# Finer interleaving slices for attention and the expert mixtures in a one-core hybrid scan kernel

## The chip, the cores and the metric

The kernel runs on one core of one Trainium2 chip. The metric is the device time of one execution in microseconds, the median of several runs. The engines are called PE (TensorE), ACT (ScalarE), DVE (VectorE), POOL (GpSimd) and SP (SyncE, which here only issues DMAs).

## The reference, cut to what matters

Four images of 32 x 32 tokens with 256 channels go through four layers. Each token row is called t, L is 1024 tokens per image.

```python
x = L0(x)                    # norm, 256->512, depthwise 3x3, gelu, scan with 64 states, norm, 512->256
x = L1(x)                    # 1x1, grouped 3x3, 1x1, residual
t = t + L2_attn(_ln_t(t))    # 8 heads of 32, masked softmax over scores, values, projection, norm
t = t + L2_ffn(_ln_t(t))     # mixture: 8 experts, hidden 256, top 2
t = t + L3_attn(_ln_t(t))    # projections, scan with 16 states, gate, projection
t = t + L3_ffn(_ln_t(t))     # mixture: 8 experts, hidden 512, top 2
# both scans:     h = exp(dt * A) * h + (dt * x) * B ;  y = sum over states of h * C
# both mixtures:  h = gelu(x @ w1[e] + b1[e]) ;  out += combine[:, e] * (h @ w2[e] + b2[e])
```

All experts are computed for all tokens; the weights of the experts that a token did not choose are zero.

## The kernel before, in words

**Two programs woven into one.** The scans are the backbone. `scans` walks through 1280 units of 128 rows (channel and state) by 1024 steps, in the order of the list `SCANS`: the 64-state scan of an image has 256 units, the 16-state scan has 64. Everything else (fronts, back ends, convolutions, attention, mixtures) is "side work": generators that yield after each small piece, called a tick. `STAGES` lists the side stages and the scan that each must wait for. The mixture of layer 2 and the attention lie in `middle`, the mixture of layer 3 in `last`.

**What one unit does.** All scan instructions are recorded through a helper and carry line 120 in the profile. For unit k: a DMA broadcasts the rows of dt into a tile `dA` (issued four units ahead), ACT turns it into a decay by `Exp` (two units ahead), PE spreads the input over the states into PSUM `ps_rep` (two matmuls, one unit ahead, two buffers of two banks each), DVE multiplies `ps_rep` by B in place, DVE runs the scan into `h`, and POOL multiplies `h` by C. Every second unit, PE sums the states of two units into `ps_y` (four matmuls in four column groups).

**Who decides the order.** The program is written with a manual schedule: each engine executes its instructions in the order in which the Python code records them. `scans` yields twice per unit: after the multiplication by B and after the scan. I call the time between two yields a half-unit slot; there are 2568 of them. In each slot `run` advances the side work by at most `TICKS = 2` ticks, and stops earlier when the planner's own clock of any engine is ahead of its clock of DVE. The planner keeps that clock with a table of costs (`Metered.COST`), which each recorded instruction adds to; an engine that is behind DVE by more than `LAG = 4` us is lifted. The costs that generators yield are not used: `advance` only asks whether a tick was made. If a scan needs a stage that is not finished, `need` runs side work at once, without scan units in between, until it is.

**The pipeline helper.** `pipe(items, *steps)` runs each item through its steps with an offset of one tick per step, the later step first: with two steps, a tick records step two of the item before and then step one of the item at hand, and then yields once.

**Attention.** `heads` (called once per half of the queries and pair of heads, eight times per image) pipes eight key blocks through `scores` and `values`. `scores` records six matmuls into two banks `ps_sc` and two `Exp` activations that write `p`; `values` records four matmuls in four column groups that add `p` times v, and `p` times ones, to `ps_at`. After the last block ACT copies `raw` and `sums` out of `ps_at`; after each second call DVE takes the reciprocal of `sums` and POOL multiplies.

**The mixtures.** `moe` handles 16 blocks (8 experts by 2 halves of the tokens), each with hidden items "h" and output items "o" of the block before. An "h" item fills two banks `ps_h` (four matmuls of 128 x 512) in step one; in step two ACT applies `Gelu` to both. The narrow mixture (layer 2, KH = 2) has one "h" item per block, the wide one (layer 3, KH = 4) has two. An "o" item fills one bank `ps_e` with 2 x KH matmuls of 128 x 256; its step two is two DVE operations that add into `tb`. `Gelu` and `Exp` are in different activation tables, so ACT loads a table when it goes from one to the other.

**PSUM.** The side work has three banks: tag "s" with two buffers and tag "acc" with one. `ps` hands them out in turn, so the bank of an allocation comes round again three allocations later.

Of the kernel before, what the change touches and what calls it, by code (L numbers as in the profile page):

```python
# [10 lines left out]
AF = mybir.ActivationFunctionType  # L11
# [5 lines left out]
P = 128  # L17
NB = 4
L = 1024
TB = L // P  # L20
# [104 lines left out]
class Hybrid:  # L125
# [38 lines left out]
        tag, bufs = (("s", 2), ("s", 2), ("acc", 1))[self.turn % 3]  # L164
        return self.psum.tile(list(shape), dtype, tag=tag, name=name, bufs=bufs)

    def pipe(self, items, *steps, cost=1.0):

        items = list(items)
        for tick in range(len(items) + len(steps) - 1):  # L170
            for s in reversed(range(len(steps))):
                if 0 <= tick - s < len(items):
                    steps[s](items[tick - s])
            yield cost if tick < len(items) else 0.5

    def load_vectors(self):
# [1051 lines left out]
    def heads(self, fp, raw, sums, qT, kT, v, maskT, mT, nh, hp):  # L1228

        nc = self.nc
        qs = slice(nh * 512, (nh + 1) * 512)
        c, at = hp // 2, 64 * (hp % 2)
        acc = self.psum.tile([P, 512], F32, tag="acc", name="ps_at", bufs=1)
        got = {}

        def scores(kb):
            two = [self.psum.tile([P, 512], F32, tag="s", name="ps_sc", bufs=2) for _ in range(2)]
            rows = [slice(at + 32 * i, at + 32 * i + 32) for i in range(2)]  # L1240
            for i in range(2):
                nc.tensor.matmul(
                    two[i], lhsT=kT[rows[i], c, kb * P : (kb + 1) * P], rhs=qT[rows[i], c, qs],
                    start=True, stop=False,
                )
            for i in range(2):
                nc.tensor.matmul(
                    two[i], lhsT=self.onesb[rows[i], :], rhs=mT[rows[i], c, qs],
                    start=False, stop=False,
                )  # L1250
            for i in range(2):
                nc.tensor.matmul(
                    two[i], lhsT=self.identb, rhs=maskT[:, kb, qs], start=False, stop=True
                )
            got[kb] = p = fp.tile([P, 2, 512], F32, tag="p", name="p", bufs=3)
            for i in range(2):
                nc.scalar.activation(p[:, i, :], two[i], AF.Exp)

        def values(kb):
            p = got.pop(kb)  # L1260
            for i in range(4):
                h = 2 * hp + i % 2
                nc.tensor.matmul(
                    acc[32 * i : 32 * i + 32, :],
                    lhsT=v[:, kb, h * HD : (h + 1) * HD] if i < 2 else self.ones,
                    rhs=p[:, i % 2, :],
                    start=(kb == 0), stop=(kb == TB - 1), tile_position=(0, 32 * i),
                )

        yield from self.pipe(range(TB), scores, values, cost=2.6)  # L1270
        nc.scalar.copy(raw[at : at + 64, c, :], acc[:64, :])
        nc.scalar.copy(sums[at : at + 64, c, :], acc[64:, :])

# [59 lines left out]
    def moe(self, which, b, tb):  # L1333

        nc, tc, a = self.nc, self.tc, self.a
        w1, w2, b1, hidden = (
            (a["L2_ffn_w1"], a["L2_ffn_w2"], self.vec["L2_ffn_b1"], 256) if which == 2
            else (a["L3_ffn_W1"], a["L3_ffn_W2"], self.vec["L3_ffn_b1"], 512)
        )
        KH = hidden // P  # L1340
        with tc.tile_pool(name=f"m{which}{b}", bufs=1, side="right") as op:
            xT = op.tile([P, 2, L], F32, name="xTm")
            cw = op.tile([P, TB, NEXP], F32, name="cw")

            def expert_weights(e):
                we1 = op.tile([P, 2, hidden], F32, tag="we1", name="we1", bufs=2)
                nc.sync.dma_start(we1, w1[e].rearrange("(k p) n -> p k n", p=P))
                we2 = op.tile([P, KH, C], F32, tag="we2", name="we2", bufs=2)
                nc.sync.dma_start(we2, w2[e].rearrange("(k p) n -> p k n", p=P))
                return we1, we2  # L1350

            weights = {0: expert_weights(0)}
            with tc.tile_pool(name=f"mg{which}{b}", bufs=1, side="right") as gp:
# [4 lines left out]
                ps = self.ps("ps_lg", (P, TB, NEXP))  # L1358
# [32 lines left out]
                got = {}  # L1391
# [16 lines left out]
            hidden_of = {}  # L1408
            got = {}

            def one(item):
                kind, e, g, i = item
                we1, we2 = weights[e]
                if kind == "h":
                    if i == 0:
                        hidden_of[e, g] = op.tile([P, KH, 512], F32, tag="h", name="h_m", bufs=2)
                        if g == 1 and e + 1 < NEXP:
                            weights[e + 1] = expert_weights(e + 1)
                    got[item] = two = [self.ps("ps_h") for _ in range(2)]
                    for s in range(2):  # L1420
                        f = 2 * i + s
                        self.mm(
                            two[s], lambda k: we1[:, k, f * P : (f + 1) * P], xT, 2,
                            slice(g * 512, (g + 1) * 512),
                        )
                    return
                h = hidden_of[e, g]
                got[item] = ps = self.ps("ps_e", (P, 2, C))
                for s in range(2):
                    m = 2 * i + s  # L1430
                    for f in range(KH):
                        nc.tensor.matmul(  # L1432
                            ps[:, s, :], lhsT=h[:, f, m * P : (m + 1) * P], rhs=we2[:, f, :],
                            start=(f == 0), stop=(f == KH - 1),
                        )

            def two(item):
                kind, e, g, i = item
                if kind == "h":
                    for s, ps in enumerate(got.pop(item)):  # L1440
                        f = 2 * i + s
                        nc.scalar.activation(
                            hidden_of[e, g][:, f, :], ps, AF.Gelu,
                            bias=b1[:, e * KH + f : e * KH + f + 1],
                        )
                    return
                ps = got.pop(item)
                for s in range(2):
                    m = 4 * g + 2 * i + s
                    nc.vector.scalar_tensor_tensor(  # L1450
                        tb[:, m, :], ps[:, s, :], cw[:, m, e : e + 1], tb[:, m, :],
                        ALU.mult, ALU.add,
                    )

            items = []
            blocks = [(e, g) for e in range(NEXP) for g in range(2)]
            for n in range(len(blocks) + 1):
                if n < len(blocks):
                    items += [("h", *blocks[n], i) for i in range(KH // 2)]
                if n:  # L1460
                    items += [("o", *blocks[n - 1], i) for i in range(2)]
            yield from self.pipe(items, one, two, cost=2.6 if which == 2 else 3.4)

    def route(self, gp, lg, cw, renorm):
# [266 lines left out]
```

## Time and profile before

| | us |
|---|---|
| median of 3 runs (lowest, highest) | 7107.39 (7104.26, 7117.05) |
| the profiled execution | 7124.43 |
| its span in the trace | 7122.6 |
| PE busy | 5418.5 (76%) |
| DVE busy | 5222.7 (73%) |
| POOL busy | 3651.6 (51%) |
| ACT busy | 3283.8 (46%), of which 456.7 in 356 table loads |
| mean granted PE clock | 0.805 |

The scan units run from 313.1 us to about 6710 us. The stretch from 5751 to 6343 us is the one place where `need` runs side work alone (the rest of image 3's middle stage, for the last scan), and from 6716 us to the end only mixtures and back ends are left. A row of a group shows the instruction, its count, the busy time, the mean duration of one in ns, and then the idle time of its engine just before such instructions with what ended it. In the rows by stretch, each engine's busy time is followed by the number of its instructions in brackets; then come the granted PE clock, the DMA share and GB/s.

### The profile page before, as it was taken

What the parts mean: (1) busy time and instruction counts of PE and PEld (TensorE: products, weight loads), DVE (VectorE), ACT (ScalarE), POOL (GpSimd) and SP (SyncE); (2) the same over time, 40 slices, a digit from 0 to 9 for tenths busy, and PEclk for the clock granted to TensorE, in tenths of its full rate; (3) what the DMA queues carried; (4) which work ended last, traced back from release to release, by engine and by line L of the source; (5) the groups of instructions that cost most, each with busy time, mean ns of one, the idle gap of its engine ahead of it and who ended that gap; (6) DMA issues with size and microseconds to landing.
All of it is one profiled execution on the core that took longest, in us unless ns stands there. A gap on an engine that the chain in (4) does not pass through costs nothing. (4 is left out here: it accounts for less than half of the span.)

```text
span 7122.6 us, 66100 instructions
## 1 busy us (share of the span) xinstructions
PE 5418.5 (76%) x20430; PEld 2202.8 (31%) x20516; DVE 5222.7 (73%) x4477; ACT 3283.8 (46%) x4024; POOL 3651.6 (51%) x1801
## 2 busy tenths in 40 slices
PE   6185876578897557879689668898598677866979
PEld 2020221032242022234235322243254322523556
DVE  2787898887898986789889877888899830237611
ACT  4164665234457324446547334556375332244411
POOL 1287677665557655555756554556656520045300
PEclk8585876579898577979779778888698788877989
DMA  2356666654456565446656654456666620135421
GB/s 82 82 138 165 159 177 165 173 139 112 118 134 172 162 174 130 114 115 174 175 147 165 175 144 113 115 134 175 164 166 165 161 75 1 48 95 158 117 62 33
DMA packets 395052, 939.02 MB, mean 132 GB/s; under 512 B 83268, under 2 KB 165776, under 8 KB 393040
## 3 DMA queue, kind: packets, MB, share of 16 engines
q1 hardware_dynamic: 392512, 932.10, 49.0%
q8 instruction: 172, 2.82, 0.2%
q0 software_dynamic: 2128, 2.13, 0.2%
q14 instruction: 240, 1.97, 0.1%
HBM read 844.17 MB, written 93.95 MB: 132 GB/s over the span
## 5 line engine op out<-in xcount | busy, mean ns | idle before, releaser
L120 POOL TENSOR_TENSOR h<-h,rows 128x1024 f32<-128x1024 f32 x1280 | 3026.2, 2367 | 2198.5 <-DVE h L120 1876.2
L120 DVE TENSOR_TENSOR_SCAN h<-dA,ps_rep 128x1024 f32<-128x1024 f32 x1280 | 2924.9, 2285 | 250.6 <-issue 98.6
L120 DVE TENSOR_TENSOR ps_rep<-ps_rep,rows 128x1024 f32<-128x1024 f32 x1280 | 1552.0, 1212 | 349.2 <-PE ps_rep L120 326.9
L120 ACT ACTIVATE dA<-dA,A_L_conv_A_log 128x1024 f32<-128x1024 f32 x1024 | 1156.7, 1146 | 853.2 <-DMA dA<-dt 767.9
L120 PE MATMUL ps_rep<-S,spread_L_conv_A_log 96*128 96x512 bf16 x2048 | 766.6, 464 | 893.5 <-DVE h L120 718.8
L120 PE MATMUL ps_y<-h,collect_L_conv_A_log 128*32 128x512 f32 x4096 | 767.4, 766 | 91.6 <-POOL h L120 87.7
L120 PEld LDWEIGHTS <-spread_L_conv_A_log 96*128 96x128 bf16 x2048 | 159.2, 103 | 1696.0 <-DVE h L120 1252.3
L120 PE MATMUL ps_h<-xTm,we 128*128 128x512 f32 x1280 | 594.1, 609 | 9.4 <-ACT h_m L120 9.4
L120 PE MATMUL ps_e<-we,h_m 128*128 128x256 f32 x2560 | 590.1, 382 | 10.5 <-ACT h_m L120 8.7
L120 ACT ACTIVATE p<-ps_sc 128x512 f32<-128x512 f32 x512 | 277.8, 594 | 598.1 <-PE ps_sc L120 429.6
L120 ACT ACT_TABLE_LOAD x356 | 456.7, 1283 | 195.5 <-DMA dA<-dt 123.9
L120 ACT ACTIVATE dA<-dA,A_L_attn_A_log 128x1024 f32<-128x1024 f32 x256 | 293.5, 1148 | 514.8 <-DMA dA<-dt 494.9
L120 PEld LDWEIGHTS ps_e<-we,h_m 128*128 128x128 f32 x2560 | 482.9, 190 | 136.6 <-issue 31.5
L120 PE MATMUL ps_at<-p,v 128*32 128x512 f32 x1024 | 366.8, 638 | 61.8 <-ACT p L120 53.3
L120 PE MATMUL ps_rep<-S,spread_L_attn_A_log 96*128 96x512 bf16 x512 | 190.7, 462 | 279.7 <-DVE h L120 236.5
L120 ACT ACTIVATE h_m<-ps_h,cols 128x512 f32<-128x512 f32 x320 | 209.3, 685 | 279.7 <-PE ps_h L120 278.1
L120 PEld LDWEIGHTS ps_h<-xTm,we 128*128 128x128 f32 x1280 | 246.6, 195 | 294.3 <-issue 243.0
L120 DVE SCALAR_TENSOR_TENSOR tb<-ps_e,cw,tb 128x256 f32<-128x256 f32 x448 | 192.4, 473 | 192.9 <-PE ps_e L120 192.4
L120 PE MATMUL ps_sc<-qT,kT 32*128 32x512 f32 x1024 | 310.1, 682 | 0.0
L120 PE MATMUL ps_at<-p,ones 128*32 128x512 f32 x1024 | 285.5, 638 | 0.0
L120 DVE RECIPROCAL sums<-sums 128x512 f32<-128x512 f32 x16 | 53.6, 3353 | 256.6 <-ACT sums L120 256.6
L120 PEld LDWEIGHTS ps_y<-h,collect_L_conv_A_log 128*32 128x32 f32 x4096 | 98.6, 119 | 448.7 <-issue 217.6
(406 smaller groups left out, 5689.3 us busy)
## 6 DMA issues: line engine op xcount, KB each, us to landing
dA<-dt SPq DMA_DIRECT2D x2048, 256.0 KB
dA<-dt SPq DMA_DIRECT2D x2048, 64.0 KB
we<-in_L_ffn_W_dram SPq DMA_DIRECT2D x64, 512.0 KB
parts<-parts SPq DMA_DIRECT2D x64, 384.0 KB
S<-parts SPq DMA_DIRECT2D x96, 256.0 KB
dt<-sp_r SPq DMA_DIRECT2D x64, 256.0 KB
y<-yo SPq DMA_DIRECT2D x128, 128.0 KB
y_back<-y SPq DMA_DIRECT2D x64, 256.0 KB
```

The source lines that it names most:

```text
L120: return got(*args, **kw)
```

## The change

Two things are changed; no arithmetic is.

- `pipe` gets an argument `cut`. With it, the generator also yields after each step but the first. `heads` sets it, so a tick of attention (values of the block before, then scores) becomes two ticks: values, yield, scores, yield. The yielded costs change too, which nothing reads.
- In `moe`, an "h" item fills one bank instead of two. There are twice as many "h" items, each with two matmuls and one `Gelu`.

```diff
-    def pipe(self, items, *steps, cost=1.0):
+    def pipe(self, items, *steps, cost=1.0, cut=False):
...
                 if 0 <= tick - s < len(items):
                     steps[s](items[tick - s])
+                    if cut and s:
+                        yield cost
             yield cost if tick < len(items) else 0.5
...
-        yield from self.pipe(range(TB), scores, values, cost=2.6)
+        yield from self.pipe(range(TB), scores, values, cost=1.3, cut=True)
...
-                    got[item] = two = [self.ps("ps_h") for _ in range(2)]
-                    for s in range(2):
-                        f = 2 * i + s
-                        self.mm(
-                            two[s], lambda k: we1[:, k, f * P : (f + 1) * P], xT, 2,
-                            slice(g * 512, (g + 1) * 512),
-                        )
+                    got[item] = ps = self.ps("ps_h")
+                    self.mm(
+                        ps, lambda k: we1[:, k, i * P : (i + 1) * P], xT, 2,
+                        slice(g * 512, (g + 1) * 512),
+                    )
                     return
...
-                    for s, ps in enumerate(got.pop(item)):
-                        f = 2 * i + s
-                        nc.scalar.activation(
-                            hidden_of[e, g][:, f, :], ps, AF.Gelu,
-                            bias=b1[:, e * KH + f : e * KH + f + 1],
-                        )
+                    nc.scalar.activation(
+                        hidden_of[e, g][:, i, :], got.pop(item), AF.Gelu,
+                        bias=b1[:, e * KH + i : e * KH + i + 1],
+                    )
                     return
...
-                    items += [("h", *blocks[n], i) for i in range(KH // 2)]
+                    items += [("h", *blocks[n], i) for i in range(KH)]
```

## The prediction

> **What bounds the kernel now.** I read the page's costliest groups first, for DVE, whose two operations per unit set the pace of the scans.
>
> ```profile
> L120 DVE TENSOR_TENSOR_SCAN h<-dA,ps_rep 128x1024 f32<-128x1024 f32 x1280 | 2924.9, 2285 | 250.6 <-issue 98.6
> L120 DVE TENSOR_TENSOR ps_rep<-ps_rep,rows 128x1024 f32<-128x1024 f32 x1280 | 1552.0, 1212 | 349.2 <-PE ps_rep L120 326.9
> ```
>
> A unit costs DVE 2.29 + 1.21 = 3.50 us, 3.60 with the gap between them. DVE waits 326.9 us in all for PE to spread the next input: that is all that side work bunched on PE can cost. Second, DVE's waits by stretch: image 2's attention (4253 to 4572 us), its narrow mixture, image 2's wide mixture.
>
> ```profile
> DVE ps_rep L120 <- PE ps_rep L120: 57.3, 35, 19.7
> DVE sums L120 <- ACT sums L120: 10.5, 3, 4.9
> ```
>
> ```profile
> DVE ps_rep L120 <- PE ps_rep L120: 4.3, 1, 4.3
> DVE tb L120 <- PE ps_b L120: 4.2, 2, 2.1
> DVE h L120 <- issue: 3.4, 18, 0.2
> DVE tb L120 <- PE ps_e L120: 2.1, 4, 0.9
> ```
>
> ```profile
> DVE h L120 <- issue: 10.3, 55, 0.2
> DVE ps_rep L120 <- PE ps_rep L120: 5.0, 3, 3.5
> ```
>
> The columns are total us, times, longest. Attention has the waits; the mixtures have hardly any. Third, busy time by stretch, four pieces of that attention and the two mixtures, tells why:
>
> ```profile
> 4253.00:4331.00 78.00, 62.20 (x315) 16.36 (x316) 49.02 (x28) 30.34 (x45) 33.17 (x14) 0.85 0.53 136
> 4343.00:4409.00 66.00, 64.13 (x305) 14.78 (x304) 48.97 (x30) 30.42 (x44) 32.54 (x15) 0.86 0.47 121
> 4442.00:4505.00 63.00, 61.26 (x314) 14.88 (x320) 48.81 (x29) 31.57 (x46) 38.04 (x18) 0.93 0.46 120
> 4514.00:4572.00 58.00, 56.15 (x303) 13.72 (x302) 48.95 (x30) 30.31 (x44) 32.59 (x15) 1.00 0.49 124
> 4656.00:4817.00 161.00, 155.88 (x610) 84.89 (x608) 147.52 (x141) 100.31 (x100) 82.65 (x35) 0.96 0.53 139
> 5156.00:5484.00 328.00, 314.69 (x1279) 168.08 (x1278) 306.54 (x233) 215.61 (x211) 193.72 (x82) 0.98 0.60 158
> ```
>
> After the length come PE, its weight loads, DVE, ACT and POOL. In attention PE is busy 97% (64.13 of 66, 56.15 of 58); the first piece also holds a wait for the mask's DMA. DVE waits there because PE has more work per unit than DVE, not because the work lies badly. In the wide mixture DVE is busy 306.5 of 328 us, and 10.3 more are fixed gaps.
>
> **What the Trainium skill says.** "Perfetto Trace Analysis", Identifying the Most-Contended Engine, calls matmul busy time a bad measure, because matmuls are pipelined. So I checked starts in the timeline: from 4514 us on, values take 1.02 us, scores 1.9, the spread 0.6 to 0.7, each starting where the one before stops issuing, with gaps of 0.5 us only where values follow their own scores at once. PE is full there. "ScalarE: Activation LUTs", What ACT_TABLE_LOAD costs, gives about 1283 ns plus a drain of about 1380 ns for a switch. The trace has 1283 ns; at 5300.75 us a load is followed at 5302.04 by a decay, with no room for that drain, so I take 1.283. "PSUM — Partial Sum Buffer", Specifications, has 8 banks of 512 fp32 values; spread (4), y (1) and side work (3) fill them, so the change can't deepen a ring. The trace does not show banks.
>
> **The change, part by part.** I followed the planner's rule through both built programs and compared their orders.
>
> (a) *Pace of side work.* The tick limit binds in 649 slots instead of 443, but work per unit is still set by the planner's PE clock. The stages start and end in nearly the same slots: image 0's middle ends in slot 920 instead of 918, image 1's in 1432 (1430), image 2's in 2072 (2070); the forced run begins at slot 2407 in both. So each of three attentions has one more scan unit beside it. Where PE is the bound, a unit adds only its PE work, 0.60 us of spread and half of 1.06 us of y, 1.13 us; elsewhere it costs 3.60. 3 x (3.60 - 1.13) = **-7.4 us**. Bounds 0 and -10.
>
> (b) *Bunching in attention.* PE's work between two spreads, counted from the built orders with the durations above, has the same mean and the same spread before and after (standard deviation 1.1 us): peaks of 7 to 8 us become 6, but units with under 3 us rise from 9 to 25. As PE is the bound, only its own idle time can go, 8.9 us per image before spreads (waiting for DVE). The reciprocals still come one slot after the last values, so their 10.5 us stay. I take **0**; bounds -27 (all three images) and +10.
>
> (c) *Values straight after their scores.* A cut lets the planner put both into one slot. Then nothing covers the two Exps (0.59 us each) and PE stands, the spread queued behind it, DVE behind that. In the built orders this happens 7 times per interleaved image before, 10 after. PE's row for it in the attention of image 2:
>
> ```profile
> L120 PE MATMUL ps_at<-p,v 128*32 128x512 f32 x252 | 89.4, 653 | 12.0 <-ACT p L120 9.4
> ```
>
> The three images show 3.7, 7.6 and 9.4 us: 20.7 for 21 cases, 0.99 each. 9 more are **+8.9 us**. Bounds 0 and +18.
>
> (d) *Bunching in the mixtures.* The standard deviation of PE's work per unit falls from 1.87 to 1.52 us (narrow) and 1.59 to 1.43 (wide). What DVE can gain is its waits: 4.3 + 2.1 in each of three narrow mixtures, 5.0 in two wide ones, 14.6 in the third (6528 to 6707 us): 44 us in all. The narrow one's 4.3 is a single wait, and a fall of the spread by 10 to 19% leaves most; I take a quarter, **-11 us**. Bounds 0 and -35.
>
> (e) *Table loads.* One Gelu instead of two per switch: the built order of ACT has 605 loads instead of 467, all 138 more in the five interleaved mixtures and their edges (64 to 98 in a wide one, 32 to 48 in a narrow one). That is 138 x 1.283 = 177 us on ACT. What hides it: ACT is busy 215.6 of 328 us in the wide mixture, 259 with 34 more loads. Queued behind a load is the next decay; DVE waits for that. Pairing the n-th decay with the n-th scan of the trace, nine decays in ten end at least 7.1 us ahead of their scan there (median 10.0), at least 7.9 in the narrow one, but 3.9 in the last wide one. One or two loads fit. I take **0**; without that cover all 177 us come onto the path. Bounds 0 and +40, the second rival's figure.
>
> (f) *Forced run and tail.* There the order on each engine is unchanged, only what is left differs: 114 half ticks of attention instead of 60 whole ones (0.35 tick less done, some 4.3 us each: +1.5), and in the last interleaved mixture 7.8 blocks instead of 8 (0.17 x 13.8 us: -2.4). **-0.9 us**. SP's and POOL's queues keep their order but for a slot here or there; the DMAs of dA and the mask are issued in the same units.
>
> Sum: -7.4 + 0 + 8.9 - 11 + 0 - 0.9 = -10.4 us. Against the profiled execution (7124.4 us, span 7122.6) that is 7114; this execution ran 17 us above the median of 7107.4, and I carry the difference over: **7097 us**.
>
> **The rivals.** *First: bunching was what counted.* For it: 326.9 us of DVE waits for spreads, and smaller pieces let PE reach the spread sooner. Against: PE is 97% busy there. If PE's idle time before spreads vanishes (-27) and half of the mixtures' waits do (-22), with (a) and (c): -7 - 27 + 9 - 22 = -47, **7060 us**.
>
> *Second, the slower one: ACT becomes the bound of the wide mixtures.* ACT's own waits in that stretch:
>
> ```profile
> ACT dA L120 <- DMA dA<-dt: 63.1, 31, 4.4
> ...
> ACT h_m L120 <- PE ps_h L120: 30.7, 21, 11.1
> ```
>
> A decay at the head of ACT's queue waits for its rows, and a Gelu behind it can't pass. If these waits do not shrink when ACT gets more work, ACT needs 215.6 + 43.6 + 63.1 + half of 30.7 = 338 of 328 us; with the 6.8 us in which loads wait for rows, 344. That is 16 us over in each of two and a half wide mixtures, +40; with the rest of the sum, -10: **7137 us**. It decides once the decays' lead of 7 to 10 us is used up. Against it: a later ACT finds its rows landed, so the waits should be what shrinks.
>
> *Third: no effect,* PE and DVE both being full: 7107 us; it is within the forecast's own range.
>
> **How the numbers follow.** Forecast with its range of 7080 to 7112: 0.55, of which 0.14 faster by more than 0.2% (below 7093, about what a measurement of this kernel can tell from no change), 0.41 within. First rival 0.28, all faster. Second 0.17, of which 0.15 slower, 0.02 within. So faster 0.42, same 0.43, slower 0.15. The range leaves out a third of the first rival (beyond its 7060) and most of what lies above the middle of the second: 7060 to 7127.
>
> **What would show it.** (a) attention in the three images over 30 slots per pair of calls, mean unit time unchanged or lower. (b) DVE's waits for spreads in attention still 40 us or more per image; under 30 speaks for the first rival. (c) PE's idle time before values up by some 3 us per image. (d) waits for spreads in the mixtures slightly down. (e) some 490 table loads instead of 356, DVE's waits for dA in the mixtures below 3 us; 10 us or more per wide mixture speaks for the second rival. I am wrong outright if the granted PE clock in the attention moves, since PE's time there scales with it, or if DVE's idle time in a mixture grows.

## The result and the profile after

The changed kernel takes 7060.53 us (median of 4 runs, 7055.46 to 7061.6) against 7112.22 us for the kernel before (4 runs, 7104.26 to 7122.82). The ratio is 0.9925, with a 95% interval of 0.9908 to 0.9942: 52 us faster, where 10 were forecast. The spans of the two profiled executions differ by 7122.6 - 7059.5 = 63 us. The profiled execution of the kernel before lay 12 us above the median of its runs, with a granted PE clock of 0.89 in image 2's attention and 0.90 in the forced run; the same orders of instructions ran there at up to 0.92 and 0.94 in other profiles. So some 10 us of the 63 are not the change's.

These groups of the page of the changed kernel answer to the first two lines of the prediction. The third is its row of table loads.

```profile
L120 DVE TENSOR_TENSOR_SCAN h<-dA,ps_rep 128x1024 f32<-128x1024 f32 x1280 | 2924.7, 2285 | 228.0 <-issue 94.6
L120 DVE TENSOR_TENSOR ps_rep<-ps_rep,rows 128x1024 f32<-128x1024 f32 x1280 | 1553.0, 1213 | 338.7 <-PE ps_rep L120 317.0
...
L120 ACT ACT_TABLE_LOAD x494 | 633.8, 1283 | 174.7 <-DMA dA<-dt 115.0
```

DVE's waits for spreads over the whole kernel fell only from 326.9 to 317.0 us. That is a fifth of the time that was gained. The loads are there: 494 in this row, 138 more than before's 356 (with those recorded at other lines the traces have 605 and 467, the counts of the built orders).

DVE's waits in the stretches of the prediction, now at image 2's attention (4222 to 4536 us), its narrow mixture and its wide one (total us, times, longest):

```profile
DVE ps_rep L120 <- PE ps_rep L120: 46.3, 46, 15.5
DVE sums L120 <- ACT sums L120: 13.5, 3, 7.9
```

```profile
DVE tb L120 <- PE ps_e L120: 4.0, 1, 4.0
DVE h L120 <- issue: 2.8, 13, 0.5
DVE tb L120 <- PE ps_b L120: 1.6, 2, 1.0
DVE ps_rep L120 <- PE ps_rep L120: 1.4, 1, 1.4
```

```profile
DVE h L120 <- issue: 8.6, 46, 0.2
DVE ps_rep L120 <- PE ps_rep L120: 7.3, 3, 4.7
```

In the narrow mixture the one wait for a spread is gone (the 1.4 us lie just before its first matmul) and the wait for `ps_e` grew from 2.1 to 4.0 us; in the wide one the waits for spreads grew by 2.3 us. The busy times of four stretches of the changed kernel (length, then PE, weight loads, DVE, ACT, POOL, clock, DMA share, GB/s) are image 0 from its last scores to its mixture, image 2's attention, and the two mixtures:

```profile
1896.60:1979.60 83.00, 46.66 (x184) 22.46 (x181) 69.17 (x94) 33.60 (x46) 44.08 (x23) 0.64 0.40 105
4222.00:4536.40 314.40, 277.83 (x1414) 77.04 (x1414) 237.45 (x147) 147.87 (x215) 157.87 (x70) 0.90 0.48 124
4618.40:4767.60 149.20, 147.71 (x590) 81.25 (x590) 140.93 (x132) 123.81 (x117) 80.71 (x35) 0.99 0.56 147
5111.30:5424.70 313.40, 305.15 (x1248) 163.49 (x1247) 295.77 (x223) 258.30 (x243) 187.70 (x80) 1.00 0.61 162
```

The first two in the kernel before:

```profile
1894.40:1984.50 90.10, 54.82 (x190) 24.32 (x191) 72.83 (x94) 32.54 (x45) 43.96 (x23) 0.57 0.40 103
4251.50:4573.60 322.10, 281.11 (x1386) 71.31 (x1412) 237.46 (x147) 147.11 (x214) 157.67 (x70) 0.89 0.47 120
```

The stretch after attention, which the prediction did not look at, became 7.1 us shorter with the same 94 DVE instructions and 23 POOL instructions, and DVE's busy time in it fell by 3.66 us. DVE does nearly the same operations in less time. Cut at the same landmarks of each trace (the mixtures from their first matmul to their last), images 0 / 1 / 2, with the time in which DVE is idle (length less DVE's busy time) behind each length:

| stretch (us) | before | after |
|---|---|---|
| attention, first to last scores | 301.4 (65.5) / 312.2 (74.9) / 322.1 (84.6) | 298.9 (62.5) / 310.0 (73.3) / 314.3 (76.9) |
| last scores to the mixture | 90.1 (17.3) / 90.1 (17.6) / 90.1 (17.6) | 82.9 (13.8) / 84.9 (15.2) / 82.0 (12.6) |
| narrow mixture | 150.4 (10.9) / 150.3 (10.9) / 150.8 (11.3) | 149.7 (8.6) / 149.0 (8.0) / 149.3 (8.3) |
| from there to the next attention | 635.2 (92.3) / 928.7 (126.8) / 935.1 (132.9) | 626.1 (85.4) / 922.6 (122.6) / 925.1 (125.8) |
| in the second and third of these, the wide mixtures | 314.5 (19.1) / 314.4 (19.0) | 312.8 (17.1) / 313.4 (17.6) |

A moved border can hand a piece of a unit to the next stretch, so idle time compares better than length. Attention loses 12 us of it by these two profiles; over several profiles of each order it became 8 us shorter in all (three attentions took 924.1 to 935.7 us in four profiles with before's order there, mean 929.7, and 920.5 to 923.2 in three with the changed one, mean 921.7). The stretch after it became 20 us shorter, the narrow mixtures lost 8.2 us of idle time, and the rest 18.2, of which 3.4 in the two wide mixtures. With -8 for attention that is -55.

**What moved.** I followed the planner's rule through the programs again, this time for single instructions. In image 1 attention's last tick is in slot 1236 before and 1237 after, the norm and the router that follow start in 1245 and 1246, the mixture runs from 1264 to 1332 and from 1265 to 1333, and the steps of layer 3 are in slots 1387, 1389, 1392, 1393 and 1389, 1391, 1393, 1395. An even slot lies between a unit's multiplication and its scan, an odd one after the scan. The step is small, but it puts the norm, the router and the start of the mixture on the other side of the scan, and it draws apart two steps of layer 3 that had stood in neighbouring slots. It comes from a detail of the cut: in the last tick of `pipe` only the values are left, and with `cut` that tick yields twice. Its second half is empty: one tick in 17 that records nothing.

### The profile page after: what moved, and what is told of

It reads as the page before. It is cut to its first block, busy times and chain, and to the rows that moved or that the text cites. A ratio compares the mean times of both kernels' runs of the same rounds, so it can differ in the third digit from the quotient of the medians.

```text
span 7059.5 us, 66331 instructions
## 1 busy us (share of the span) xinstructions
PE 5383.6 (76%) x20516; PEld 2218.2 (31%) x20516; DVE 5212.0 (74%) x4477; ACT 3462.1 (49%) x4162; POOL 3650.0 (52%) x1801
## 5 line engine op out<-in xcount | busy, mean ns | idle before, releaser
L120 DVE TENSOR_TENSOR_SCAN h<-dA,ps_rep 128x1024 f32<-128x1024 f32 x1280 | 2924.7, 2285 | 228.0 <-issue 94.6
L120 DVE TENSOR_TENSOR ps_rep<-ps_rep,rows 128x1024 f32<-128x1024 f32 x1280 | 1553.0, 1213 | 338.7 <-PE ps_rep L120 317.0
L120 PE MATMUL ps_y<-h,collect_L_conv_A_log 128*32 128x512 f32 x4096 | 750.2, 755 | 91.1 <-POOL h L120 91.1
L120 PE MATMUL ps_at<-p,v 128*32 128x512 f32 x1024 | 363.6, 627 | 63.1 <-ACT p L120 55.7
```

The lines of the kernel that those rows point to most:

```text
L120: return got(*args, **kw)
```

## The experiments

The two theories are called **P**, place (what counts is which slots later steps fall into, moved by the empty tick), and **G**, grain (what counts is that the pieces are smaller).

**1 and 2. Each part alone.** `attn_only` keeps the cut and puts the mixtures back; `mix_only` the reverse.

> The attention part alone: values and scores in ticks of their own, the mixtures as before. Theory P (place): the gain comes from where the work after attention falls, because the cut leaves one empty tick at the end of each call and so moves everything up to the end of the middle stage one to two slots later; here the same shift happens, so about -20 us after attention (7 per image), -13 in the steps of layer 3, -7 for one more unit beside side work: -40 us, 0.9944. Theory G (granularity): smaller pieces let PE serve the scans sooner; then only the attention's own share shows, -12 us and nothing elsewhere: 0.998. On record before: +1.5 us (-7.4 and +8.9).

> The mixtures' part alone, attention as before. The slots after attention stay where they were, the narrow mixture ends one slot later and the steps of layer 3 fall where they fall in the changed kernel. Theory P: nothing after attention, -14 in the narrow mixtures and -13 in the steps: -25 us, 0.9965. Theory G: the smoother mixtures gain in both widths, wide ones 5 us each: -25 us too, but in the mixtures and not in the steps. On record before: -11 us for it. The rival with ACT as the bound: slower by 20 us or more.

Measured: attention's part 7058.06 against 7111.62 us, 0.9920 (0.9907 to 0.9934); the mixtures' part 7089.25, 0.9967 (0.9955 to 0.9979). Attention's part alone gives all of the gain. The two do not add up: -54 and -22 alone, -52 together. With the mixtures' part alone the mixture ends one slot later and the steps of layer 3 stand in 1388, 1391, 1393, 1395; the stretch after attention stays at 90.2 us, and DVE's idle time from the narrow mixture's end to the next attention falls by 15.8 us in three images, as by the other part alone (15.3). So it seems to move what the other part moves anyway; **Open**, below, comes back to this.

**3. The cut without its empty tick.** Mixtures as before:

```diff
-                    if cut and s:
+                    if cut and s and tick < len(items):
                         yield cost
```

> Attention cut as in the change, but without the empty tick that the cut leaves at the end of each call, so that everything after attention falls into the slots of before; the mixtures as before. Theory P: what the cut itself does is nearly nothing, -5 to +5 us, 0.9995 to 1.0005. Theory G: -12 us or more, as in attention alone. On record before: +8.9 us from values that follow their scores at once.

Measured: 7141.9 against 7111.62, **1.0044** (1.003 to 1.0058). The same fine pieces, slots after attention as before, and it is slower by 30 us. G fails here, but so does P's number: attention itself took 312.6 / 321.9 / 323.6 us, some 10 us per image more than the mean of the profiles with before's order. That needed a cause of its own (see 9).

**4. The empty ticks without the cut.** The kernel before, with two ticks that record nothing at the end of each half of the queries:

```diff
                         yield from self.heads(fp, raw, sums, qT, kT, v, maskT, mT, nh, hp)
+                        if hp == 3:
+                            yield 0.5
+                            yield 0.5
```

> The kernel before with two empty ticks after the last reciprocal of each half of the queries, and nothing else: attention whole, mixtures whole, but what follows falls into the slots of the changed kernel. Theory P: -20 us after attention, -13 in the steps, and about -7 for the unit more: -35 to -40 us, 0.995, which is most of what the change brings. Theory G: nothing, or the cost of the empty ticks: 1.000 to 1.001.

Measured: 7043.83 against 7111.62, 0.9904 (0.9889 to 0.9919). Ticks that record nothing gain as much as the whole change (0.9904 against 0.9925; the intervals overlap), and on the same chip more than `attn_only` (7040.76 to 7047.44 against 7048.59 to 7063.15). The stretch after attention took 83.3 / 83.7 / 83.7 us and the attentions 298.4 / 305.2 / 308.3. More than expected, since attention shrank as well. This has the lowest ratio of all that ran, and beats both kernels' times.

**5. The empty ticks later.** Two of them in `middle`, between attention and the mixture, so that attention's own back end keeps its slots and only the norm, the router and what follows move.

```diff
             yield from self.attention(b, tb)
+            yield 0.5
+            yield 0.5
             yield from self.moe(2, b, tb)
```

> The kernel before with two empty ticks between attention and the narrow mixture of each image, nothing else: the mixture's norm and routing, the mixture and the steps fall into the slots of the changed kernel, but the projection and norm at the end of attention stay where they were. If the whole tail after attention gains from its place: 3 to 4 of the 7 us per image there, the unit more beside the mixture (-4 us per image) and the steps: -25 to -35 us, 0.996. If the gain after attention comes from the last projection and norm alone: -15 us, 0.998.

Measured: 7068.21 against 7113.86, 0.9934 (0.9921 to 0.9947). The stretch shrank to 84.1 us. Two thirds of the gain of experiment 4 come with norm, router and what lies after: 46 us, more than the 25 to 35 that were expected.

**6. What the place changes: POOL left out.** The kernel before, with POOL's multiplication of `h` by C left out in three groups of 15 units, beside the stretch after each attention (C is missing there; all else is computed):

```diff
-                nc.gpsimd.tensor_tensor(h, h, Cm, ALU.mult)
+                if not any(lo <= k < lo + 15 for lo in (362, 618, 938)):
+                    nc.gpsimd.tensor_tensor(h, h, Cm, ALU.mult)
```

> The kernel before, with the multiplication by C on GpSimd left out for the 15 scan units beside the end of each attention and the routing of the narrow mixture (so the y of these units lacks its factor C); all slots as before. If the small DVE operations there are slow because GpSimd works on SBUF at the same time, the four or five that take 1 to 2 us take some 0.2 us, and the stretch from the last scores to the mixture's first matmul shrinks from 90 us by about 7 us, as the moved slots do. If they are slow for another reason (a queue, a semaphore), they stay at 1 to 2 us and the stretch at 90 us.

It was read by its stretch, not by its time (a single run, 7072.8 us). The busy times of the stretch:

```profile
1897.00:1977.10 80.10, 50.22 (x190) 20.91 (x191) 65.50 (x94) 32.41 (x45) 11.26 (x9) 0.62 0.45 116
```

The slots are before's, yet it takes 80.1 instead of 90.1 us, and DVE is busy for 65.50 instead of 72.83 us. These are DVE's groups by shape in that stretch, of the kernel before:

```profile
L120 DVE TENSOR_TENSOR ps_rep<-ps_rep,rows 128x1024 f32<-128x1024 f32 x14 | 17.0, 1213 | 4.2 <-PE ps_rep L120 4.2
...
L120 DVE TENSOR_TENSOR tb<-ps_b,tb 128x512 f32<-128x512 f32 x4 | 2.7, 682 | 4.2 <-PE ps_b L120 4.2
L120 DVE TENSOR_TENSOR r_one<-lg,r_one_m 128x64 f32<-128x64 f32 x1 | 2.0, 2010 | 0.0
L120 DVE TENSOR_SCALAR lny_v<-lny_mv 128x4 f32<-128x4 f32 x1 | 2.0, 1951 | 0.0
L120 DVE TENSOR_TENSOR lnm_w<-lnm_r 128x8 f32<-128x8 f32 x1 | 1.9, 1891 | 0.6 <-ACT lnm_r L120 0.6
L120 DVE TENSOR_TENSOR lg<-lg,r_mx 128x64 f32<-128x64 f32 x1 | 1.3, 1309 | 0.0
...
L120 DVE TENSOR_REDUCE r_mx<-lg 128x8 f32<-128x64 f32 x1 | 0.2, 207 | 0.0
```

Of the changed kernel:

```profile
L120 DVE TENSOR_TENSOR ps_rep<-ps_rep,rows 128x1024 f32<-128x1024 f32 x14 | 17.0, 1217 | 2.6 <-PE ps_rep L120 2.6
...
L120 DVE TENSOR_TENSOR r_two<-r_rest,r_two_m 128x64 f32<-128x64 f32 x1 | 2.2, 2160 | 0.0
L120 DVE TENSOR_TENSOR tb<-ps_b,tb 128x512 f32<-128x512 f32 x3 | 2.1, 688 | 1.6 <-PE ps_b L120 1.6
...
L120 DVE TENSOR_TENSOR r_one<-lg,r_one_m 128x64 f32<-128x64 f32 x1 | 0.9, 932 | 0.0
...
L120 DVE TENSOR_TENSOR lg<-lg,r_mx 128x64 f32<-128x64 f32 x1 | 0.2, 227 | 0.0
...
L120 DVE TENSOR_SCALAR lny_v<-lny_mv 128x4 f32<-128x4 f32 x1 | 0.2, 170 | 0.0
...
L120 DVE TENSOR_TENSOR lnm_w<-lnm_r 128x8 f32<-128x8 f32 x1 | 0.2, 166 | 0.6 <-ACT lnm_r L120 0.6
```

And without POOL's work:

```profile
L120 DVE TENSOR_TENSOR r_one<-lg,r_one_m 128x64 f32<-128x64 f32 x1 | 0.2, 225 | 0.0
L120 DVE TENSOR_TENSOR r_two<-r_rest,r_two_m 128x64 f32<-128x64 f32 x1 | 0.2, 225 | 0.0
```

An operation on 4 to 64 elements per partition takes 0.15 to 0.23 us alone and up to 2.2 us next to POOL. The timeline of the kernel before shows why (start, duration), DVE first and then POOL:

```profile
1936.04 0.15 DVE L120 TENSOR_SCALAR lnm_v<-lnm_mv 128x8 f32<-128x8 f32 x1
1936.76 1.89 DVE L120 TENSOR_TENSOR lnm_w<-lnm_r 128x8 f32<-128x8 f32 x1 [0.58 <-ACT lnm_r L120]
1938.68 0.17 DVE L120 TENSOR_TENSOR lnm_w<-lnm_w,lnm_v 128x8 f32<-128x8 f32 x1
```

```profile
1936.27 2.36 POOL L120 TENSOR_TENSOR h<-h,rows 128x1024 f32<-128x1024 f32 x1 [2.40 <-DVE lnm_v L120]
```

POOL starts half a microsecond earlier and ends at 1938.63; the small operation, 1936.76 + 1.89, ends at 1938.65. It stood until POOL was done. "SBUF — State Buffer" of the Trainium skill, Who interferes with whom, says just this: a DVE instruction with two inputs in SBUF, or in a 2-port mode, which `tensor_scalar` can enter, shares a port pair with GpSimd as an exclusive lock; the one issued second blocks until the first ends. The traces agree: the reduction `r_mx`, with its single input, takes 207 ns in the kernel before though it lies (at 1958.89) within a POOL multiplication (1958.00 to 1960.36), while the operation right after it, `lg<-lg,r_mx`, takes 1309 ns and ends with POOL; and the two large operations of a unit, whose `ps_rep` lies in PSUM, keep their 2285 and 1213 ns. POOL starts when the scan ends. So an operation just after the scan (odd slot) pays up to 2 us; one that comes after the next multiplication has 1.1 us or more of that behind it, as `lg<-lg,r_mx` has, which lost 1.1 us. (The 0.7 us of the changed kernel's `r_one` were lost to another POOL operation, of 1.27 us.) In all, the small operations of this stretch lose 7.2 us in each image before and 3.5, 4.6 and 4.2 after.

That is the smaller half of what this stretch gained. Over the three images it became 20.5 us shorter, and DVE's busy time fell by 9.6 of these. The other 10.9 are idle time, mostly shorter waits for PE, such as those for `ps_rep` and `ps_b` in the rows above. Experiment 5 shows the two apart: its stretch is 6.0 us shorter, with only 0.8 us less of busy time. These waits go with the slots, too, but what shortens each of them was not isolated. Leaving POOL out shortened one of them as well: of its 10.0 us, 7.3 are busy time and 2.7 idle time, the wait for the spread.

**7. The grain inside the mixtures.** `paired` is the changed kernel with Gelus applied two at a time after every second hidden item, so that only the loads go back (356 in its page); `phase_mix` is experiment 4 with the mixtures' part added.

```diff
+                    if i % 2 == 0:
+                        return
+                    for f in (i - 1, i):
+                        nc.scalar.activation(
+                            hidden_of[e, g][:, f, :], got.pop((kind, e, g, f)), AF.Gelu,
+                            bias=b1[:, e * KH + f : e * KH + f + 1],
+                        )
```

> The changed kernel, but the Gelus of the mixtures applied two at a time after every second hidden item: one bank a tick on PE, 467 table loads in the program instead of 605, all slots of the changed kernel. If the 138 loads more are hidden, as recorded before the result: the time of the changed kernel, 0.992 to 0.993. If they cost something: 10 to 20 us less than the changed kernel, 0.990.

> Two empty ticks after the last reciprocal of each half of the queries, attention whole, and the mixtures' first layer one bank a tick. If the mixtures' part adds a gain of its own to the moved slots: below the kernel with the empty ticks alone (0.9904), 0.988. If its gain alone (0.9967) was also only the moved end of the narrow mixture and the steps, which the empty ticks move already: the same as the empty ticks alone, 0.990 to 0.991.

Measured: `paired` 7049.69 against 7113.86, 0.9909 (0.9895 to 0.9924); `phase_mix` 7048.63, 0.9908 (0.9895 to 0.9922). The ratio of `paired` lies nearer to 0.990, which was expected if the loads cost something, than to 0.992. But its interval overlaps the change's; of the 12.8 us between the two profiles 4.9 lie before the first attention, where the programs do not differ; and its mixtures take the same time: narrow 149.1 / 148.7 / 149.3 us against 149.7 / 149.0 / 149.3, wide 314.0 / 313.4 / 287.2 against 312.8 / 313.4 / 285.5. Neither the 138 loads nor their absence shows there. And to the slots of experiment 4 (0.9904) the mixtures' part adds nothing that the times show.

**8. The whole change without its empty tick.** The edit of experiment 3 in the changed kernel; both parts stand.

> The changed kernel without the empty tick at the end of each attention call: both parts of the change stand, but what follows attention stays in the slots of before until the narrow mixture ends. Theory P: attention 11 us longer per image, as with the cut alone in these slots (+33), nothing gained after attention, and the mixtures' part as alone (-22): +11 us, 1.0015, so the change would not have paid. Theory G: the pieces are as small as in the changed kernel, so its gain stays: 0.992 to 0.994.

Measured: 7119.74 against 7105.53, **1.0020** (1.0011 to 1.0029). One condition, which decides about a tick that records nothing, separates 0.9925 from 1.0020. The three attentions take 312.8 / 322.3 / 322.8 us, the stretch after the first of them 89.7: both losses are back. P is confirmed by its number, 1.0015; G expected 0.992 to 0.994.

**9. Attention itself: the place of the sums over states.** Why did the cut without the empty tick lengthen attention? I measured the time from one group of scores to the next at full granted clock, by what PE does in between. In the kernel before:

```profile
4514.55 1.13 PE L120 MATMUL ps_sc<-qT,kT 32*128 32x512 f32 x4
...
4516.97 1.10 PE L120 MATMUL ps_at<-p,v 128*32 128x512 f32 x3 [0.53 <-ACT p L120]
...
4518.44 1.13 PE L120 MATMUL ps_sc<-qT,kT 32*128 32x512 f32 x4
...
4520.16 0.60 PE L120 MATMUL ps_rep<-S,spread_L_conv_A_log 96*128 96x512 bf16 x2
4520.86 1.10 PE L120 MATMUL ps_at<-p,v 128*32 128x512 f32 x3
...
4522.33 1.13 PE L120 MATMUL ps_sc<-qT,kT 32*128 32x512 f32 x4
...
4524.14 1.07 PE L120 MATMUL ps_y<-h,collect_L_conv_A_log 128*32 128x512 f32 x8
4525.14 0.60 PE L120 MATMUL ps_rep<-S,spread_L_conv_A_log 96*128 96x512 bf16 x2
...
4526.67 1.13 PE L120 MATMUL ps_sc<-qT,kT 32*128 32x512 f32 x4
```

Scores and values alone: 4518.44 - 4514.55 = 3.89 us. With a spread put in between: 4522.33 - 4518.44 = 3.89 as well. The spread is free, because the values wait for the second Exp. With the sums `ps_y` and then a spread: 4526.67 - 4522.33 = 4.34. In the kernel of experiment 3 the sums come in another place:

```profile
2887.56 1.13 PE L120 MATMUL ps_sc<-qT,kT 32*128 32x512 f32 x4
...
2889.28 0.60 PE L120 MATMUL ps_rep<-S,spread_L_attn_A_log 96*128 96x512 bf16 x2
2889.97 1.11 PE L120 MATMUL ps_at<-p,v 128*32 128x512 f32 x3
...
2891.29 1.09 PE L120 MATMUL ps_y<-h,collect_L_attn_A_log 128*32 128x512 f32 x7
2892.31 1.13 PE L120 MATMUL ps_sc<-qT,kT 32*128 32x512 f32 x4
```

Here they follow the values, no wait covers them, and the cycle is 4.75 us. The medians are the same in all kernels: 3.89 without `ps_y`, 4.10 with spread, then `ps_y`, then values; 4.34 with `ps_y` first; 4.75 with `ps_y` after the values. What differs is how often each comes. Over three images, at full clock, the kernel before has 53 cycles of 4.34 and 18 of 4.10; the changed one 59 of 4.10 and a few with two spreads; experiment 3 has 54 of 4.75 and 17 of 4.10, 18 per image that cost 0.41 to 0.65 us more, 7 to 12 us. That is most of its 10 us. With all kinds of cycle counted at their medians, three attentions of the changed kernel cost some 10 us less than before's, and those of experiment 3 some 31 more; measured, by the means over profiles, were 8 less and 28 more.

To try it the other way I recorded the sums of a pair before the first slot of a unit instead of between its slots, and once more with the empty ticks of experiment 4:

```diff
+            if k % 2 == 1 and 2 <= k < len(units) + 2:
+                pair(k - 2)
...
-            if k % 2 == 1 and 2 <= k < len(units) + 2:
-                pair(k - 2)
```

> The kernel before with the sum over states recorded before the first yield of a unit instead of before the second (so PE has it straight after the spread); values then follow their own scores at once 24 times per interleaved image instead of 7. Read in the attention's stretch (300, 311, 314 us before in undisturbed profiles), since slots elsewhere move too. As on record, 0.99 us for each such case: 17 more per image, attention 15 us longer or more. From the cycles counted in the traces (scores to scores at full clock: 3.89 us with or without a spread between, 4.10 with the sum after the spread, 4.34 with it before, 4.75 with it after the values): these cases cost nothing and the sums cost less, attention 0 to 5 us shorter per image.

> The same with the two empty ticks after the last reciprocal of each half of the queries. If the two gains add, it beats the empty ticks alone (0.9904): 0.988. The end of attention falls as in the changed kernel, but routing and steps start in the slots of before, so some of the gain of the place may be lost: 0.992.

Measured: 7115.81 against 7105.53, 1.0012 (1.0004 to 1.0020), and 7070.78, 0.9948 (0.9930 to 0.9966). The first is a miss: I had expected it no slower. Attention took 308.9 / 321.0 / 320.6 us. The move put two spreads and the sums between the same scores and values, at 4.77 us, and values came straight after scores 24 times per image instead of 7. At the prediction's 0.99 us per case those 17 more would have been 17 us per image, and it was 8. So the list of cycles tells what each order costs, but not by itself which orders a shift will produce; at its medians it gives 12 of the 21 us by which the three attentions grew over the mean of before's order.

## Why the prediction was wrong

**(a) Pace of side work is the step that failed.** It says that the stages "start and end in nearly the same slots", and prices the difference of one or two slots as scan units that come to lie beside attention, 3 x (3.60 - 1.13). But every instruction of those stages moved by one or two slots, many of them to the other side of the scan, and the step gave that no price. The units beside attention are not more either: there are 147 DVE instructions in image 2's attention before and after. The one unit more came beside the narrow mixture (34 POOL instructions before, 35 after). What the moved slots were worth: -20 us in the stretch after attention (experiments 4, 5 and 8; a little under half of it is the lock of experiment 6), -8 in attention, by where the sums fall (the account of cycles), about -8 of idle time in the narrow mixtures (10.9 to 11.3 us each before, 7.7 to 8.0 with the empty ticks alone and mixtures as before; there a single wait for a spread, 4.1 to 4.3 us before, fell to 0.6 or 0.7, and that for `ps_e` grew from 1.8 to 3.1), and about -15 in the steps of layer 3 and what follows them (-18.2 less the wide mixtures' 3.4). Together that is some -50 us, where the step had -7.4. Of the last part the main piece can be seen: DVE's waits for ACT in image 1's steps, in the kernel before and then in the changed one.

```profile
DVE sp_x L120 <- ACT parts L120: 12.7, 4, 5.2
DVE sp_e L120 <- ACT sp_l L120: 7.9, 1, 7.9
```

```profile
DVE sp_x L120 <- ACT parts L120: 7.8, 4, 2.7
DVE sp_e L120 <- ACT sp_l L120: 6.5, 1, 6.5
```

Two steps stood in neighbouring slots, 1392 and 1393, and stand two apart now, so the second has more time for its ACT result to come: 20.6 us of waits became 14.3. The traces of the other runs show that this goes with the slots and not with the pieces. Over the three images these waits sum to 62.4 us before, 45.3 in the changed kernel and 44.1 with the empty ticks alone, but 62.7 with the cut without its empty tick. Other waits in that stretch grew and shrank, so that the net is some 15.

**(b) Bunching in attention, 0.** Right as to grain: the waits for spreads stayed over 40 us, 57.3 to 46.3. Its reason, "PE is the bound", was wrong, and with it the price of 1.13 us per unit in (a). The cycle is a chain: scores, two Exps, values. PE looks 97% busy in it, and still takes a spread for nothing. The prediction had the hint in its hands ("Perfetto Trace Analysis" of the Trainium skill, Identifying the Most-Contended Engine, calls matmul busy time a bad measure of PE) and tested it by starts alone; comparing the period with and without a spread would have told.

**(c) Values straight after their scores, +8.9.** Not found. PE's idle time before image 2's values went from 9.4 to 7.8 us, where 3 us more were forecast; over the three images it went from 20.7 to 21.4:

```profile
L120 PE MATMUL ps_at<-p,v 128*32 128x512 f32 x252 | 88.0, 642 | 10.0 <-ACT p L120 7.8
```

The gap is real, 0.53 us in the timeline, but it is the wait that the spread otherwise fills; the cycle is 3.89 us both ways. A case costs what the spread then does elsewhere: in the `y_early` kernel 8 us for 17 cases, some 0.5 each if all of it is theirs, which was not separated.

**(d) Bunching in the mixtures, -11.** Too large. By DVE's idle time, smaller pieces alone (`mix_only`) gave 1.4, 1.0 and 2.0 us in the narrow mixtures and 1.6 and 0.6 in two wide ones. Where the slots had moved already, the narrow ones gave nothing (`attn_only` 7.7 to 8.2 us, the whole change 8.0 to 8.6), and only the wide ones are left: 18.7 to 18.8 us against 17.1 to 17.6, some 3 us in two; the third took 284.2 us before and 285.5 after. The narrow one's single wait for a spread, of which this step took a quarter for the pieces, is 2.4 to 2.6 us with the pieces alone, and 0.6 to 0.7 with the place alone.

**(e) Table loads, 0.** Right, as far as these runs can tell (experiment 7). There are 494 loads for 490 forecast, and the cover did what was said of it: in the wide mixture ACT went from 214.4 of 314.4 us to 258.3 of 313.4, and its waits for rows shrank from 63.1 to 10.4 us:

```profile
ACT h_m L120 <- PE ps_h L120: 43.6, 22, 8.5
ACT dA L120 <- DMA dA<-dt: 10.4, 6, 3.3
```

The decays' median lead fell from 10.0 to 6.8 us, and the wide mixtures stayed within 1.7 us. **The second rival** fails by that: the waits are what shrank.

**(f) Forced run and tail, -0.9.** Nothing speaks against it; the forced attention took 288.8 us before and 283.2 after, but 281.0 and 279.6 in other kernels with before's order there, at a higher granted clock.

**The first rival** named 7060, the measured time, and was still not what happened. It needed 49 us from waits for spreads. The page shows 10, the empty ticks alone gained as much with these waits at 326.8 us, as before, and with the same grain and no empty tick the gain is gone.

**Open.** Why `attn_only` is some 14 us slower than the empty ticks alone on the same chip: 9 us of it lie in its attentions, the rest was not found. Nor was it isolated what shortens DVE's waits for PE after attention. The mixtures' part alone gains its 22 us largely by the same steps of layer 3: their waits for ACT sum to 34.5 us there, 28 less than before, and to 34.1 in experiment 8. Why the two parts together keep 45.3 was not followed further than to the slots: these steps start in slot 1388 with the mixtures' part alone and in 1389 with both.

## What to carry to other kernels

In a schedule that is written out by hand, an edit that only regroups work also moves all that follows; follow the first instructions of the next stages to their new slots, and price what lies beside them there. To tell whether it is the grain or the place that counts, move the place alone with an empty step, and change the grain with the places held. Before calling an engine full, look for the same cycle with one instruction more and one fewer: if its length is the same, the bound is a chain of waits.

## What the runs showed of the hardware

- A DVE operation on two SBUF inputs of 4 to 64 elements per partition took 0.16 to 0.23 us, and (seen with 8 and 64) 1.9 to 2.2 us when it was issued just after a POOL multiplication of 2.36 us had started. That is nearly as much as a scan of 1024 steps, 2.29 us. In the profile it shows as a long operation, not as a wait.
- In the cycle of scores, two Exps and values (3.89 us) a spread of 0.60 us is free. In a cycle with a spread, sums of some 1.07 us cost 0.21, 0.45 or 0.86 us more, as they come after the spread, before it or after the values.
- Executions of the same order of instructions differed by 9 us in one attention of some 315, with the granted clock (322.1 us at 0.887 in the kernel before; 312.8 us at 0.915 in `mix_only`). A difference smaller than that can't be read from one such stretch of two single profiles.
